# A transformer block on one core: GpSimd zeroes the exponentials of later keys in place of masks in the scores

## The chip, the core and the metric

The kernel runs on one core of one Trainium2 chip. The time is the device time in microseconds. The engines are TensorE (PE, matrix products; PEld is its weight load), VectorE (DVE), ScalarE (ACT), GpSimd (POOL) and SyncE (SP, which issues most DMAs). Each works through its own instructions in order; semaphores hold an instruction back until what it needs is done. Matrix products are written to PSUM, 8 banks here used as three pairs (`mring`) and two singles (`accp`).

## The reference

The input is x of 4 x 2048 tokens and 256 channels. A small conditioning product gives shifts, scales and gates. Then:

```python
h = _layernorm(x, axis=-1) * (1 + ca) + sa
x = x + ga * _L0_attn_ref(h, ...)        # 8 heads of 32 channels
h = _layernorm(x, axis=-1) * (1 + cb) + sb
x = x + gb * _L0_ffn_ref(h, ...)         # 2 shared and 16 routed experts, 4 per token
```

and in the attention, what bears on the change:

```python
scores = jnp.where(causal[None, None], scores, -jnp.inf)
scores = scores + head_scales[None, :, None, None] * geo
attn = jax.nn.softmax(scores, axis=-1)
out = jnp.einsum('bhqk,bhkd->bqhd', attn, v)
```

A query sees its own key and earlier ones. The extra term `geo` is a product of a projection of q and one of k, which the kernel folds into the key weights.

## The kernel before, in words

Queries are taken in 16 blocks of 512 (`QB`), four blocks to a sequence; block i has place qb = i % 4 in its sequence, so it meets qb + 1 blocks of keys. Heads are taken in two groups of four (`NQ`), and the four heads of a group lie in the four row or column quarters of TensorE, so their products run side by side.

Attention goes over the scores twice. First come the maxima (`max_steps`, lines 418 to 474), always one block ahead: `ps` is scores with queries on partitions, VectorE adds `cmask` to its last 128 columns and takes row maxima into `parts`; these are negated, cut into three bf16 pieces and turned into `mT` by TensorE (`pr`).

Then come the sums (`sum_steps`, lines 663 to 750), tile by tile of 128 keys (`kb`). `probabilities(kb)` computes `st`, scores with keys on partitions, into two pairs of PSUM banks, two heads in each, and adds the negated maxima by a product with `unit3`. In the last four key tiles, those on the diagonal, keys later than a query must vanish: there, in lines 702 to 710, four more products of `ident_b` with `kmask` (-1e30 where the key is later) are added to 128 columns of each head. A diagonal tile is computed from column `lo` on only, so the four are 512, 384, 256 and 128 columns wide. ScalarE takes the exponential of each pair into its half of `pt` (lines 711 to 714). `weigh(kb, s)` (lines 716 to 733) multiplies these with the values into `av` and with ones into `dv`, summed over all key tiles in the two `accp` banks. After the last tile `finish` (lines 735 to 741) copies `av` out on ScalarE (`num`) and `dv` on VectorE (`rd`), takes the reciprocal of 128x512 and multiplies, giving `oT`. `out_steps` (line 752) multiplies `oT` with the output weights.

The order of work is written out by hand. Every engine but for a few scatters keeps the order in which the program calls it (class `Pinned`, line 41; every operation is therefore recorded at line 52, and groups are told apart by the names of their tiles). In the stage of sums each step has a place on an axis counted in key tiles, and `run` sorts by it (lines 1404 to 1456):

```python
for n, (first, average, total) in enumerate(sums):
    part.append((n, first))
    part.append((n + 1.3, average))
    part.append((n + 1.6, total))
```

so TensorE takes the scores of tile n+1 ahead of the weighing of tile n. At n + 0.5 stand maxima of the next block, at n + 0.8 pieces of the expert choice, of the second layer norm (`second_norm_steps`, line 802) and of the next first norm, at n + 0.9 a `tick`. A norm has a power of -0.5 on GpSimd (`rsb`, waiting for VectorE), four scalings on VectorE (`xnb`), and eight multiplications or additions on GpSimd (`modulate`, line 807) with a store to `h2d` from GpSimd's queue behind them. A `tick` issues one indirect DMA from GpSimd: a scatter of a row tile to its experts' places (`xg`) or a gather back (`got`); each waits for the last instruction that ScalarE had been given (`paced`, line 496). Between two stages of sums, `fill_in` (line 515) interleaves projections (`pta`, `ppq`, `ppk`, `pv`), the turned hidden states (`ptb`), the shared experts (`pu_-2`, `pd_s`), the routed experts' tiles (`px`, `pu`, `py`) and more maxima with estimated durations; `tail` places the output products (`po`) last. After block 15 the last two blocks go through all experts densely, between the last routed tiles (lines 1464 to 1499).

Of the kernel before, what the change touches and what calls it, by code (L numbers as in the profile page):

```python
# [92 lines left out]
def adaln_block_kernel(  # L93
# [103 lines left out]
    for k in range(KC):  # L197
# [5 lines left out]
    make_identity(tc.nc, ident)  # L203
    cmask = const.tile([P, P], F32, tag="cmask", name="cmask")
    make_causal_mask(tc.nc, cmask, MASK)
    kmask = const.tile([P, P], BF16, tag="kmask", name="kmask")
    nc.gpsimd.memset(kmask, 0.0)
    nc.gpsimd.affine_select(
        out=kmask,
        in_=kmask,  # L210
        pattern=[[1, P]],
        compare_op=ALU.is_ge,
        fill=MASK,
        base=0,
        channel_multiplier=-1,
    )
    ident_b = const.tile([P, P], BF16, tag="ident_b", name="ident_b")
    nc.vector.tensor_copy(ident_b, ident)
    c_pair = cmask.unsqueeze(1).broadcast_to([P, 2, P])
# [325 lines left out]
    def merged(one, other):  # L545

        placed = []
        for pieces in (one, other):
            at, total = 0.0, sum(us for us, _ in pieces)
            for us, step in pieces:  # L550
                placed.append(((at + us / 2) / total, (us, step)))
                at += us
        return [p for _, p in sorted(placed, key=lambda p: p[0])]
# [102 lines left out]
        left = fill_in(merged(project_steps(2), gates_to_come[4:]), tops[:10])  # L656
        rest = tops[10:]

    probs = ctx.enter_context(tc.tile_pool(name="probs", bufs=2))
    tiles = ctx.enter_context(tc.tile_pool(name="tiles", bufs=2))  # L660
    kept = ctx.enter_context(tc.tile_pool(name="kept", bufs=3))

    def sum_steps(i, g, oT):

        qb = i % NB
        nkb = (qb + 1) * TT
        qT, mT = qTs[i], mTs[i, g]
        sums = []
        pts = {}

        def keys(kb):
            return (i - qb + kb // TT) % SLOTS, kb % TT

        def left(kb):
            return max(0, kb - qb * TT) * P

        def probabilities(kb):
            lo = left(kb)
            slot, n = keys(kb)
            halves = [pair(f"st{i}_{g}_{kb}_{a}") for a in range(2)]  # L680
            heads = [both[:, u, :] for both in halves for u in range(2)]
            for h in range(4):
                r = G * h
                nc.tensor.matmul(
                    heads[h][:, lo:],
                    lhsT=kT[r : r + G, slot, g, n * P : (n + 1) * P],
                    rhs=qT[r : r + G, g, lo:],
                    start=True,
                    stop=False,
                    tile_position=(r, 0),  # L690
                )
            for h in range(4):
                r = G * h
                nc.tensor.matmul(
                    heads[h][:, lo:],
                    lhsT=unit3[r : r + 3, :],
                    rhs=mT[r : r + 3, lo:],
                    start=False,
                    stop=(kb < qb * TT),
                    tile_position=(r, 0),  # L700
                )
            if kb >= qb * TT:
                for h in range(4):
                    nc.tensor.matmul(
                        heads[h][:, lo : lo + P],
                        lhsT=ident_b,
                        rhs=kmask,
                        start=False,
                        stop=True,
                    )  # L710
            pt = probs.tile([P, 4, QB], F32, tag="pt", name=f"p{i}_{g}_{kb}")
            for a, both in enumerate(halves):
                nc.scalar.activation(pt[:, 2 * a : 2 * a + 2, lo:], both[:, :, lo:], AF.Exp)
            pts[kb] = pt

        def weigh(kb, s):
            if kb == 0:
                sums.append(accp.tile([P, QB], F32, tag="acc", name=f"{'ad'[s]}v{i}_{g}"))
            lo = left(kb)
            slot, n = keys(kb)  # L720
            for h in range(4):
                r = G * h
                c0 = g * P + r
                nc.tensor.matmul(
                    sums[s][r : r + G, lo:],
                    lhsT=ones if s else vA[:, slot, n, c0 : c0 + G],
                    rhs=pts[kb][:, h, lo:],
                    start=(kb == 0),
                    stop=(kb == nkb - 1),
                    tile_position=(0, r),  # L730
                )
            if s and kb == nkb - 1:
                finish()

        def finish():
            rd = once.tile([P, QB], F32, tag="rd", name=f"rd{i}_{g}")
            num = once.tile([P, QB], F32, tag="num", name=f"num{i}_{g}")
            nc.scalar.copy(num, sums[0])
            nc.vector.tensor_copy(rd, sums[1])
            nc.vector.reciprocal(rd, rd)  # L740
            nc.vector.tensor_tensor(oT[:, g, :], num, rd, ALU.mult)

        return [
            [
                lambda kb=kb: probabilities(kb),
                lambda kb=kb: weigh(kb, 0),
                lambda kb=kb: weigh(kb, 1),
            ]
            for kb in range(nkb)
        ]  # L750

    def out_steps(i, oT):

# [208 lines left out]
    def place_steps(group):  # L962
# [18 lines left out]

        def owners():
            shape = [P, MAXT, R]
            past = once.tile(shape, BF16, tag="num", name=f"past{n}")
            nc.vector.tensor_tensor(
                past,
                tile_no.unsqueeze(2).broadcast_to(shape),
# [352 lines left out]
    def free(steps):  # L1340
        return [(0.001, s) for s in steps]

    oT = None
    filled = None
    for i in range(NBLK):
        b, qb = i // NB, i % NB
# [3 lines left out]
        if i:  # L1350
# [17 lines left out]
                mid = turns[:2] + ups + turns[2:]  # L1368
            if soon and later:
                mid += project_steps(later[0])  # L1370
            ends = [s for two in zip(downs, outs) for s in two] if downs else outs
            at = max(6, len(mid) - len(ends))
            tail = merged(mid[at:], ends) if mid[at:] else ends
            mid = mid[:at] + tail
            tops = [] if last else maxima(i + 1)
            state["pairs"] = not last
            own = sum(us for us, _ in lead + mid)
# [23 lines left out]
        if i == 0:  # L1401
            load_gates(0)
        oT = once.tile([P, KC, QB], F32, tag="oT", name=f"oT{i}")
        sums = [s for g in range(NQ) for s in sum_steps(i, g, oT)]
        assert len(sums) == ks
        part = []
        for n, (first, average, total) in enumerate(sums):
            part.append((n, first))
            part.append((n + 1.3, average))
            part.append((n + 1.6, total))  # L1410
        for n, (_, ss, turn) in enumerate(rest):
# [69 lines left out]
    more, much, others = dense_steps(j)  # L1481
    choice = free(choice_steps(i, None))
    outs = out_steps(j, oT)
    begin = turn_steps(i) + outs[:1] + choice[:2] + outs[1:] + ups
    begin += choice[2:3] + downs[:1] + choice[3:] + downs[1:] + free(second_norm_steps(j))
    fill_in(begin + in_turn(pairs[:1]), pace=1.3, add=True)
    while scatters:
        tick()
    tiles_of(filled)
    choice = free(choice_steps(j, None))  # L1490
    late = turn_steps(j) + choice + more
    rest = take_tiles(1e9)
    amid = in_turn(pairs[1:6])
    fill_in(merged(rest[:30], amid[:9]) + merged(rest[30:], amid[9:] + late), pace=2.4, add=True)
    fill_in(in_turn(pairs[6:]) + much + in_turn(others), pace=1.6, add=True)
    while ready or sums_due:
        tick()
# [44 lines left out]
```

## Time and profile before

| | us |
|---|---|
| median of 3 runs (lowest, highest) | 2557.42 (2553.51, 2558.43) |
| the profiled execution | 2559.8 |
| its span, first to last instruction | 2558.1 |
| stage of sums, block 7 (16 key tiles, two groups) | 990.7 to 1101.1 |
| end of the last stage of sums | 2281.8 |

Work by kind, from the groups of the profile (busy us):

| TensorE | | other engines | |
|---|---|---|---|
| st, scores for the sums | 421.0 | VectorE, row maxima | 662.4 |
| ps, scores for the maxima | 387.8 | ScalarE, exponentials | 538.4 |
| av and dv | 312.5 and 303.3 | GpSimd, gathers | 219.5 |
| the maxima added to st | 162.3 | GpSimd, scatters | 213.2 |

In the profile's lines, a group is named line, engine, operation, out<-in, shape and count; then busy time, mean ns of one, and the idle time of the engine just before these instructions with what ended it. A timeline's line has start and length in us first. "PEclk" is the granted share of TensorE's clock. The mean clock of the profiled execution was 0.954.

### The profile page before, as it was taken

The numbers are of one execution on the slowest core, as the hardware profiler recorded it, in microseconds if no ns is written. First come the engines' busy times: TensorE is split into PE (matmuls) and PEld (weight loads), VectorE is DVE, ScalarE is ACT, GpSimd is POOL, SyncE is SP. The second block draws the span as 40 slices with busy tenths as digits, with TensorE's granted clock in tenths as the row PEclk, the third lists the DMA queues.
The fourth block names the chain that finished last, engine by engine and source line by source line (L and its number), as shares of the span: only waits on it lengthen the run. The fifth ranks groups of instructions, "written<-read, shape, count | busy, mean of one in ns | idle before, by whom it ended". The sixth has DMA issues, their size and how long they took to land.

```text
span 2558.1 us, 42345 instructions
## 1 busy us (share of the span) xinstructions
PE 2386.6 (93%) x16961; PEld 1165.1 (46%) x16961; DVE 1405.7 (55%) x2609; ACT 977.6 (38%) x1372; POOL 701.4 (27%) x740
## 2 busy tenths in 40 slices
PE   7999999999999899999999999999898999997987
PEld 4443424345554223355654335254545643345754
DVE  5576665526666855347565566346664564422235
ACT  2223233543433234544343344643344345542320
POOL 3201010411133144202015332401442025543234
PEclk9889899999999899999999999998999999998999
DMA  2300401434432112223742235233636843247943
GB/s 87 118 1 9 148 9 42 153 127 149 154 118 63 44 58 81 75 75 101 228 136 79 73 108 173 75 101 100 214 122 215 260 144 98 89 145 264 313 135 111
DMA packets 219701, 306.90 MB, mean 120 GB/s; under 512 B 18544, under 2 KB 158832, under 8 KB 219504
## 3 DMA queue, kind: packets, MB, share of 16 engines
q1 hardware_dynamic: 192720, 228.89, 27.4%
q0 software_dynamic: 25536, 73.43, 9.1%
q8 instruction: 134, 2.20, 0.4%
q10 hardware_dynamic: 1248, 1.86, 0.2%
q14 instruction: 63, 0.52, 0.1%
HBM read 193.49 MB, written 114.82 MB: 121 GB/s over the span
## 4 chain that ended last, share of the span: by engine, by line
PE 75%; DVE 12%; ACT 4%; issue 4%; POOL 2%; DMA 2%; SPq 0%; POOLq 0%; ACTq 0%; DVEq 0%
PE st L52 15%; PE ps L52 12%; PE av L52 9%; PE dv L52 8%; PE pu L52 7%; PE py L52 5%; DVE parts L52 4%; PE po L52 3%; PE ppq L52 2%; PE pv L52 2%; PE px L52 2%; PE ppk L52 2%; DVE rd L52 2%; PE pd_s L52 1%; PE pd L52 1%
## 5 line engine op out<-in xcount | busy, mean ns | idle before, releaser
L52 DVE TENSOR_REDUCE parts<-ps 128x2 f32<-128x1024 f32 (+3 forms) x640 | 662.4, 1062 | 348.6 <-PE ps L52 339.6
L52 ACT ACTIVATE p<-st 128x1024 f32<-128x1024 f32 (+3 forms) x640 | 538.4, 893 | 652.8 <-PE st L52 652.5
L52 PE MATMUL st<-qT,kv 32*128 32x512 f32 (+3 forms) x2560 | 421.0, 594 | 32.8 <-DVE parts L52 21.0
L52 PE MATMUL ps<-kv,qT 32*128 32x512 f32 (+3 forms) x2560 | 387.8, 608 | 16.9 <-DVE parts L52 9.7
L52 POOL DMA_INDIRECT got<-yg,at x224 | 219.5, 980 | 399.7 <-ACT p L52 134.1
L52 PE MATMUL av<-p,kv 128*32 128x512 f32 (+3 forms) x2560 | 312.5, 561 | 4.6 <-DVE rd L52 4.6
L52 PE MATMUL dv<-p,ones 128*32 128x512 f32 (+3 forms) x2560 | 303.3, 546 | 0.0
L72 POOL DMA_INDIRECT xg<-rows,at x219 | 213.2, 974 | 266.9 <-ACT p L52 109.7
L52 PEld LDWEIGHTS st<-qT,kv 32*128 32x128 f32 x2560 | 141.0, 189 | 295.8 <-issue 209.2
L52 DVE TENSOR_TENSOR ps<-ps,cmask 128x256 f32<-128x256 f32 x256 | 109.3, 427 | 266.3 <-PE ps L52 245.9
L52 PEld LDWEIGHTS ps<-kv,qT 32*128 32x128 f32 x2560 | 127.8, 192 | 207.1 <-issue 112.9
L52 POOL TENSOR_TENSOR x<-x,tmps 128x512 f32<-128x512 f32 x28 | 35.4, 1263 | 623.1 <-DVE tmps L52 623.0
L52 PE MATMUL py<-wt,tact 128*128 128x256 f32 x608 | 163.8, 403 | 7.7 <-ACT xt L52 3.5
L52 PEld LDWEIGHTS pu<-xt,wt 128*128 128x128 f32 x1216 | 150.5, 197 | 29.5 <-issue 11.5
L52 PE MATMUL pu<-xt,wt 128*128 128x128 f32 x1216 | 158.3, 284 | 4.8 <-DMA wt<-experts 3.7
L52 PE MATMUL st<-mT,unit 3*128 3x512 bf16 (+3 forms) x1280 | 162.3, 353 | 0.0
L52 PEld LDWEIGHTS dv<-p,ones 128*32 128x32 f32 x2560 | 74.0, 111 | 173.9 <-issue 167.0
L52 DVE SCALAR_TENSOR_TENSOR sum<-got,weight,sum 128x256 f32<-128x256 f32 x168 | 82.9, 494 | 123.3 <-DMA got<-yg,at 119.5
L52 ACT COPY y<-py 128x512 f32<-128x512 f32 x152 | 89.0, 586 | 155.0 <-PE py L52 154.4
L52 PEld LDWEIGHTS py<-wt,tact 128*128 128x128 f32 x608 | 109.8, 195 | 57.6 <-issue 15.2
L52 ACT COPY xt<-px 128x512 f32<-128x512 f32 x152 | 86.9, 586 | 101.1 <-PE px L52 100.5
L52 PEld LDWEIGHTS av<-p,kv 128*32 128x32 f32 x2560 | 53.8, 109 | 140.1 <-issue 118.7
(287 smaller groups left out, 2425.9 us busy)
## 6 DMA issues: line engine op xcount, KB each, us to landing
wt<-experts SPq DMA_DIRECT2D x304, 256.0 KB, 4.3
xr<-xg SPq DMA_DIRECT2D x76, 512.0 KB, 4.6
yg<-y SPq DMA_DIRECT2D x76, 512.0 KB, 3.5
xg<-zeros SPq DMA_DIRECT2D x16, 1024.0 KB, 10.0
xin<-in_x SPq DMA_DIRECT2D x16, 512.0 KB, 6.2
x<-in_x SPq DMA_DIRECT2D x16, 512.0 KB, 4.5
h2d<-xnb POOLq DMA_DIRECT2D x14, 512.0 KB
pre<-x POOLq DMA_DIRECT2D x14, 512.0 KB, 3.4
```

The lines of the kernel that those rows point to most:

```text
L52: made = call(*args, **kwargs)
L72: made = call()
```

## The change

1. `kmask` and its four products in each diagonal tile are gone. In their place GpSimd sets the exponentials of later keys to 0 in SBUF: `mask(kb)` runs one `affine_select` for each half of a diagonal tile, on 128 partitions by two heads by 128 columns, 256 in all, at place n + 0.7.
2. The probabilities of a tile are two tiles of two heads each, in 5 buffers, where there was one of four heads in 2 buffers. The experts' activations, which share the tag `pt`, have 5 buffers too.
3. The order of key tiles: the first three diagonal tiles each stand ahead of a third of the other tiles, and the fourth is last. In blocks with qb = 0 there are diagonal tiles only.
4. The copies `num` and `rd` are issued at the last weighing of each, and reciprocal and product come in four pieces of 128 columns: for the first head group among the second one's tiles, for the second among the first pieces of the following fill.
5. `past` takes a buffer of tag `y` in place of `num`'s.
6. At the end, after block 15, the second norm of the last block comes behind the remaining scatters instead of ahead of them, and the last block's choice has its first step ahead of the shared experts' first products and its others behind.

The diff, cut to its core:

```diff
@@ -656,7 +645,7 @@
-    probs = ctx.enter_context(tc.tile_pool(name="probs", bufs=2))
+    probs = ctx.enter_context(tc.tile_pool(name="probs", bufs=5))
...
+        full, edge = list(range(qb * TT)), list(range(qb * TT, nkb))
+        order = edge
+        if qb:
+            cut = [0, (len(full) + 2) // 3, (2 * len(full) + 2) // 3, len(full)]
+            order = [k for n in range(3) for k in edge[n : n + 1] + full[cut[n] : cut[n + 1]]]
+            order += edge[3:]
...
-            if kb >= qb * TT:
-                for h in range(4):
-                    nc.tensor.matmul(
-                        heads[h][:, lo : lo + P],
-                        lhsT=ident_b,
-                        rhs=kmask,
-                        start=False,
-                        stop=True,
-                    )
-            pt = probs.tile([P, 4, QB], F32, tag="pt", name=f"p{i}_{g}_{kb}")
+            pts[kb] = []
             for a, both in enumerate(halves):
-                nc.scalar.activation(pt[:, 2 * a : 2 * a + 2, lo:], both[:, :, lo:], AF.Exp)
-            pts[kb] = pt
+                pt = probs.tile([P, 2, QB], F32, tag="pt", name=f"p{i}_{g}_{kb}_{a}")
+                nc.scalar.activation(pt[:, :, lo:], both[:, :, lo:], AF.Exp)
+                pts[kb].append(pt)
+
+        def mask(kb):
+
+            lo = left(kb)
+            for pt in pts[kb]:
+                nc.gpsimd.affine_select(
+                    out=pt[:, :, lo : lo + P],
+                    in_=pt[:, :, lo : lo + P],
+                    pattern=[[0, 2], [1, P]],
+                    compare_op=ALU.is_ge,
+                    fill=0.0,
+                    base=0,
+                    channel_multiplier=-1,
+                )
...
-            if s and kb == nkb - 1:
-                finish()
...
+            if last and s:
+                held["rd"] = once.tile([P, QB], F32, tag="rd", name=f"rd{i}_{g}")
+                nc.vector.tensor_copy(held["rd"], sums[1])
+            elif last:
+                held["num"] = once.tile([P, QB], F32, tag="num", name=f"num{i}_{g}")
+                nc.scalar.copy(held["num"], sums[0])
+
+        def divide(t):
+            own = slice(t * P, (t + 1) * P)
+            rd = held["rd"]
+            nc.vector.reciprocal(rd[:, own], rd[:, own])
+            nc.vector.tensor_tensor(oT[:, g, own], held["num"][:, own], rd[:, own], ALU.mult)
...
+            for n, s in enumerate(ends):
+                (lead or mid).insert(2 * n + 1, (0.001, s))
...
+        part = [(ks // NQ + 1.05 + 0.8 * n, s) for n, s in enumerate(divided)]
+        for n, (first, mask, average, total) in enumerate(sums + more):
             part.append((n, first))
+            if mask is not None:
+                part.append((n + 0.7, mask))
             part.append((n + 1.3, average))
             part.append((n + 1.6, total))
...
-    begin += choice[2:3] + downs[:1] + choice[3:] + downs[1:] + free(second_norm_steps(j))
+    begin += choice[2:3] + downs[:1] + choice[3:] + downs[1:]
...
-    late = turn_steps(j) + choice + more
+    norms = second_norm_steps(j)
+    turns = turn_steps(j)
+    late = turns + choice[:1] + more + choice[1:]
...
-    fill_in(merged(rest[:30], amid[:9]) + merged(rest[30:], amid[9:] + late), pace=2.4, add=True)
+    fill_in(free(norms) + merged(rest[:30], amid[:9]) + merged(rest[30:], amid[9:] + late), pace=2.4, add=True)
```

## The prediction

> **What bounds the kernel now.** I read the page's busy times first, then the costliest groups with shapes kept apart, then the gaps of TensorE (the waits by engine, the timeline around them, and the granted clock there), and last GpSimd's queue.
>
> ```profile
> PE 2386.6 (93%) x16961; PEld 1165.1 (46%) x16961; DVE 1405.7 (55%) x2609; ACT 977.6 (38%) x1372; POOL 701.4 (27%) x740
> ...
> PEclk9889899999999899999999999998999999998999
> ...
> PE 75%; DVE 12%; ACT 4%; issue 4%; POOL 2%; DMA 2%; SPq 0%; POOLq 0%; ACTq 0%; DVEq 0%
> ```
>
> TensorE is busy 93% of the span and is 75% of the chain that ended last; its own gaps between matmuls sum to 145 us in the trace. GpSimd is busy 27%. So a matmul taken away is worth its issue time, and a new wait in TensorE's stream costs its length. The groups that the change touches:
>
> ```profile
> L52 PE MATMUL st<-kmask,ident_b 128*128 128x128 bf16 x512 | 51.8, 225 | 0.0
> ...
> L52 DVE RECIPROCAL rd<-rd 128x512 f32<-128x512 f32 x32 | 107.3, 3353 | 1.1
> ...
> L52 POOL TENSOR_TENSOR xnb<-xnb,gm 128x256 f32<-128x256 f32 x128 | 93.9, 746 | 16.5 <-DVE xnb L52 5.2 <-issue 5.2 <-PE av L52 0.6
> ...
> masks.py:30 POOL TENSOR_SCALAR_AFFINE_SELECT cmask<-cmask 128x128 f32<-128x128 f32 x1 | 0.3, 287 | 0.0
> ```
>
> The first row is what goes. It is never waited for (idle before it 0.0), so it stands in the dense stream. The timeline of TensorE at one diagonal tile shows its real price:
>
> ```profile
> 1036.84 0.40 PE L52 MATMUL st<-mT,unit 3*128 3x512 bf16 x4
> 1037.16 0.40 PE L52 MATMUL st<-kmask,ident_b 128*128 128x128 bf16 x4
> 1037.49 1.06 PE L52 MATMUL av<-p,kv 128*32 128x512 f32 x8
> ```
>
> From 1037.16 to 1037.49 is 0.33 us; busy time overlaps its neighbours, so 0.33 and not 0.40 is what is saved.
>
> **The change part by part.**
>
> *Masks out of the scores.* 128 diagonal tiles (16 blocks, 2 head groups, 4 tiles), 0.33 us from the first mask matmul to the next instruction, near the same each time: 42.9 us of TensorE. All of it is on the path. Diagonal exponentials start 0.33 us sooner; that is not counted again.
>
> *256 selects on GpSimd.* No row shows 128x2x128. The same operation took 287 ns on 128x128; doubled, 0.57 us. Taking off the 98 ns that a one-element memset takes on GpSimd gives 0.48. I take 0.5: about 1 us for a tile's two, 128 us in all on an engine that is idle 73% of the time. That by itself costs nothing. What can cost is that av now waits for GpSimd instead of ScalarE. Behind av in TensorE's queue stand dv, the next scores and everything else. The room is read where it is tightest, at the first tile of a group:
>
> ```profile
> 1049.79 1.94 ACT L52 ACTIVATE p<-st 128x1024 f32<-128x1024 f32 x2 [1.73 <-PE st L52]
> ...
> 1052.14 1.06 PE L52 MATMUL av<-p,kv 128*32 128x512 f32 x8
> ```
>
> The second exponential ends at 1051.73, av starts at 1052.14, and its matmuls on the second half at about 1052.60: 0.87 us for one select of 0.5 us. It just fits, because the halves are now tiles of their own and the first half's select runs beside the second exponential. In the middle of a group the same distance is 1.50 us or more in nine tiles of ten. So a free GpSimd costs TensorE nothing. The cover is gone where GpSimd is not free: it works in order, and selects stand behind norms, scatters and gathers. The changed program's GpSimd order shows where. In block 5 two gathers, eight xnb multiplications, the h2d store and one gather stand between the selects of the third and fourth diagonal tiles, two tiles apart. The same run of work in the trace:
>
> ```profile
> 759.51 1.54 POOL L52 TENSOR_TENSOR xnb<-xnb,gm 128x256 f32<-128x256 f32 x2
> 761.21 0.99 POOL L52 DMA_INDIRECT got<-yg,at  x1 [0.15 <-issue]
> 762.51 0.95 POOL L52 DMA_INDIRECT got<-yg,at  x1 [0.30 <-issue]
> 763.89 4.98 POOL L52 TENSOR_TENSOR xnb<-xnb,gm 128x256 f32<-128x256 f32 x6 [0.43 <-DVE xnb L52]
> 769.17 0.85 POOL L52 DMA_DIRECT2D h2d<-xnb  x1 [0.30 <-POOL xnb L52]
> ```
>
> With the third tile's selects put in and another gather after the store, the fourth tile's first select is done at about 772.4 by these durations; its av started at 768.0 in the trace: some 4 us. Block 13 has the same pattern, 4 us. In blocks 4 and 8 the rsb power waits for VectorE until 649.9 and 1203.5, with the third tile's select behind it and two xnb more ahead of the fourth's: 2.5 us each. In block 12 rsb came at 1793.2, and the last select now stands behind it; the fill after it waited 3.9 us for VectorE anyway, so 3 us net. Block 9 has two scatters ahead of the second group's first select: 1 us; block 1: 0.5. In the nine others four or five tiles lie between diagonal ones and absorb such runs: 0.7 each, 6.3. Sum 24 us. Bounds: 0 if all is absorbed, not below, since a wait can't speed TensorE; 60 if each of 32 groups loses nearly 2 us.
>
> *What a gap costs beyond itself.* Here a page and a row disagree. The Trainium skill, page "TensorE: Matmul & The Clock Gate", section "What's actually happening", lets TensorE drop to half clock after an idle window of some 3.4 us; by it a 2 us wait costs 2 us. The trace:
>
> ```profile
> 927.29 0.91 PE L52 MATMUL st<-qT,kv 32*128 32x512 f32 x2 [1.99 <-DVE parts L52]
> ```
>
> and the busy times by stretch around it (the column before the last two is the granted clock):
>
> ```profile
> 900.00:927.00 27.00, 25.19 (x228) 8.55 (x224) 14.72 (x16) 9.64 (x14) 14.78 (x17) 1.00 0.22 74
> 927.00:935.00 8.00, 7.71 (x36) 1.62 (x40) 2.77 (x5) 1.94 (x2) 0.97 (x1) 0.57 0.06 18
> ```
>
> After a gap of 1.99 us the clock is 0.57 for 8 us. There are 33 half-clock stretches, 236 us, in which st takes 1056 ns instead of 588, so 118 us are lost; over 145 us of gaps that is 0.8 us per us. I multiply gaps by 1.8: the selects' 24 us become 43; by the page they would stay 24.
>
> A second rule speaks against the change: "SBUF — State Buffer", section "SBUF: two separate sides", has VectorE's operations on two SBUF inputs and GpSimd's hold one port pair against each other for a whole instruction. The trace agrees: rpr<-log,rmx takes 224 ns, and about 1260 in 5 of 16 cases, one of them beside GpSimd's 1.25 us x<-x,tmp at 438.05. By the rule each select may hold such an operation up 0.5 us or be held up itself. The maxima read PSUM and fall outside it; selects fill a tenth of the attention's time, so I put nothing on the path and up to 15 us in the range.
>
> *Quotients in pieces.* 192 more VectorE instructions at some 160 ns of fixed cost (a reduction takes 1221 ns on 1024 elements, 693 on 512): 31 us, covered by VectorE's 45% idle time; without that cover, 1 us per group. The gain: a reciprocal of 3.35 us with its copy and product no longer holds the maxima up in one lump. Ten TensorE gaps follow these lumps (133, 374, 771, 777, 925, 1206, 1481, 1793, 2128 and 2286 us), 21.7 us in all, 39 with the clock. The copy out of PSUM stays and the sum of work grows, so I take 60%: 23 us. Bounds 0 and 39.
>
> *Diagonal tiles apart.* Narrow tiles no longer follow one another, so maxima are spread better over TensorE's time; of 20 us of other waits for parts perhaps 5 go. Counted in the range only.
>
> *At the end.* The second norm leaves the place ahead of the last four scatters. They ran at 2309.8, after 7.1 us of rsb and xnb, and px waited 9.4 us for the rows. The scatters still wait for a Gelu that ends at 2305.8: 4 to 5 us, 8 with the clock. The later choice keeps its chain of exponential, top values and gate behind the wait, so its 6.4 us gap stays.
>
> *At nothing:* five half tiles for two whole ones (each tile's reuse still lies two tiles back), past in y's buffers (5 times; a late y store would cost its few us), the earlier num copy, and the missing kmask setup (0.5 us at the start).
>
> Sum: 42.9 + 23 + 8 - 43 = 31 us off the profiled execution's 2559.8, which stands 2.4 us above the median of 2557.4: 2526.
>
> **Rivals.** *(1) GpSimd's queue becomes the bound of diagonal tiles, slower.* If av waits for a select behind norms or indirect DMAs, at 2.5 us x 1.8 = 4.5 us a time, the 74 us gained are gone at 16 such waits, one per block. At 24 waits it costs 108: 2557.4 + 34 = 2591. For it: in-order GpSimd and rsb's dependence on VectorE. Against it: in nine blocks the diagonal tiles are far apart. Chance 0.24. *(2) Smoothing doesn't come:* VectorE's waits only move, leaving 42.9 + 8 - 43 = 8 us: 2549. For it: VectorE gets no less work. Chance 0.19, nearly half of it within 0.2%. *(3) Waits are absorbed:* a stall lets VectorE catch up and stands in place of a later gap, so only 10 us of the 43 remain and the quotients give 39: 42.9 + 39 + 8 - 10 = 80, 2477. Chance 0.15. My forecast has 0.42.
>
> The range: the forecast's terms alone give 2500 to 2552; it is drawn out to rivals 1 and 3, 2484 to 2592. Faster than 0.2% (5 us, about what a measurement of this kernel can tell from no change): 0.67; within it 0.08; slower 0.25.
>
> **What would show it.** No kmask row; TensorE's busy time down by about 50 us; some 128 us of selects at 0.5 us each. "PE av <- POOL p" among the waits, 20 to 25 us, mostly in blocks 4, 5, 8, 12 and 13. Waits for rd and parts down by about 13 us. The px wait at the end near 5 us. A mean clock near 0.954. I am wrong if av's wait for GpSimd is over 40 us, or a select takes 0.8 us or more, or the mean clock falls under 0.945.

## The result, and the profile after

The changed kernel took 2587.37 us (median of 4 runs, 2581.54 to 2589.83) beside 2557.53 us of the kernel before (4 runs): a ratio of 1.0113, 95% interval 1.0092 to 1.0134. It is slower by 30 us where I had put 31 us of gain; that lies inside my range, 4 us from the 2591 of rival 1. The profiled execution is 2589.53 us with a span of 2587.8 us.

The experiments ran later, in five rounds, each on a chip of another number (0, 2, 5, 13 and 15); which chip the first pair had is not on record. There the two kernels stand closer: the changed kernel, repeated in two of the rounds, is at 1.0011 (0.9997 to 1.0026) and 1.0016 (1.0001 to 1.0032). It takes the same 2590 us there, but the kernel before has a median of 2582 to 2587 us in all five rounds. So a loss of 11 parts in a thousand was seen in the first pair alone, and where an expectation speaks of "the chip of the experiments", five are meant. Every ratio of an experiment is to runs of the kernel before in the same round, beside it; the quotient of the two medians can differ from it by up to 0.002.

From the page of the changed kernel: busy times, the granted clock in 40 slices, and the chain that ended last by engine.

```profile
PE 2391.7 (92%) x16449; PEld 1156.1 (45%) x16449; DVE 1436.2 (56%) x2801; ACT 977.8 (38%) x1372; POOL 805.4 (31%) x994
...
PEclk9889899999999899999989899998998999899999
...
PE 72%; DVE 10%; POOL 6%; issue 5%; DMA 4%; ACT 3%; SPq 0%; POOLq 0%; ACTq 0%; DVEq 0%
```

512 matmuls are gone and TensorE is busy 5 us longer, not 50 us shorter. Its gaps sum to 170.3 us (145.5 before), and the granted clock is half for 311.6 us (236.4). GpSimd has risen from 2% to 6% of the chain. The groups that answer to those shown of before:

```profile
L52 PE MATMUL av<-p,kv 128*32 128x512 f32 (+3 forms) x2560 | 336.7, 580 | 56.1 <-POOL p L52 54.4
...
L52 POOL TENSOR_SCALAR_AFFINE_SELECT p<-p 128x256 f32<-128x256 f32 x256 | 105.1, 423 | 364.3 <-ACT p L52 362.3
```

A select takes 0.42 us (I had 0.5), 105 us in all. But before av TensorE now stands still for 54.4 us, and GpSimd is what ends it. Among TensorE's waits by releaser it is the largest by far (columns: us in total, times, longest):

```profile
PE av L52 <- POOL p L52: 54.4, 21, 5.9
PE st L52 <- DVE parts L52: 11.4, 18, 2.3
PE ps L52 <- DVE parts L52: 11.1, 24, 1.6
...
PE px L52 <- DMA xr<-xg: 9.0, 2, 4.7
```

The longest is in block 15, one of those that I thought safe. The timeline of ScalarE, GpSimd and TensorE there (start, duration, instruction, idle time before it and what ended it; some instructions left out):

```profile
2249.90 0.97 POOL L72 DMA_INDIRECT xg<-rows,at  x1 [0.30 <-issue]
...
2250.88 4.51 POOL L52 TENSOR_TENSOR xnb<-xnb,gm 128x256 f32<-128x256 f32 x6
...
2252.49 1.94 ACT L52 ACTIVATE p<-st 128x1024 f32<-128x1024 f32 x2 [2.06 <-PE st L52]
2255.54 1.01 POOL L72 DMA_INDIRECT xg<-rows,at  x1 [0.15 <-issue]
2256.86 0.97 POOL L72 DMA_INDIRECT xg<-rows,at  x1 [0.30 <-issue]
2257.84 0.78 POOL L52 TENSOR_SCALAR_AFFINE_SELECT p<-p 128x256 f32<-128x256 f32 x2
2258.32 0.19 PEld L52 LDWEIGHTS av<-p,kv 128*32 128x32 f32 x4 [6.62 <-POOL p L52]
2258.32 1.43 PE L52 MATMUL av<-p,kv 128*32 128x256 f32 x8 [5.91 <-POOL p L52]
```

Six multiplications of the norm and three scatters, eight microseconds of GpSimd, stand ahead of a select of 0.4 us, and av starts 0.48 us after that select has begun. Then av takes 1.43 us where it takes 0.64 at full clock. The busy times by stretch around it (the column before the last two is the granted clock) show why:

```profile
2240.00:2250.00 10.00, 10.00 (x100) 2.81 (x96) 5.50 (x17) 6.46 (x8) 3.30 (x4) 1.00 0.08 27
2250.00:2256.00 6.00, 2.41 (x24) 0.56 (x16) 0.00 (x0) 2.38 (x3) 5.60 (x8) 0.87 0.13 44
2256.00:2266.00 10.00, 7.68 (x48) 2.39 (x52) 0.00 (x0) 1.94 (x2) 6.65 (x9) 0.57 0.19 66
```

### The profile page after: what moved, and what is told of

Its sections match the earlier page's. It is cut to its first block, busy times and chain, and to the rows that moved or that the text cites. A ratio compares the mean times of both kernels' runs of the same rounds, so it can differ in the third digit from the quotient of the medians.

```text
span 2587.8 us, 42082 instructions
## 1 busy us (share of the span) xinstructions
PE 2391.7 (92%) x16449; PEld 1156.1 (45%) x16449; DVE 1436.2 (56%) x2801; ACT 977.8 (38%) x1372; POOL 805.4 (31%) x994
## 4 chain that ended last, share of the span: by engine, by line
PE 72%; DVE 10%; POOL 6%; issue 5%; DMA 4%; ACT 3%; SPq 0%; POOLq 0%; ACTq 0%; DVEq 0%
PE st L52 12%; PE ps L52 12%; PE av L52 9%; PE dv L52 7%; PE pu L52 7%; PE py L52 5%; DVE parts L52 4%; PE po L52 3%; PE ppq L52 2%; PE pv L52 2%; PE px L52 2%; PE ppk L52 2%; POOL xnb L52 2%; POOL got L52 2%; PE pd L52 2%
## 5 line engine op out<-in xcount | busy, mean ns | idle before, releaser
L52 PE MATMUL ps<-kv,qT 32*128 32x512 f32 (+3 forms) x2560 | 399.2, 610 | 19.0 <-DVE parts L52 11.1
L52 PE MATMUL av<-p,kv 128*32 128x512 f32 (+3 forms) x2560 | 336.7, 580 | 56.1 <-POOL p L52 54.4
L52 PE MATMUL dv<-p,ones 128*32 128x512 f32 (+3 forms) x2560 | 322.6, 559 | 0.0
L52 POOL TENSOR_SCALAR_AFFINE_SELECT p<-p 128x256 f32<-128x256 f32 x256 | 105.1, 423 | 364.3 <-ACT p L52 362.3
L52 PEld LDWEIGHTS av<-p,kv 128*32 128x32 f32 x2560 | 59.0, 111 | 246.8 <-issue 161.1
L52 PEld LDWEIGHTS dv<-p,ones 128*32 128x32 f32 x2560 | 84.5, 115 | 180.7 <-issue 172.6
```

The costliest lines, as they stand in the source:

```text
L52: made = call(*args, **kwargs)
```

## The experiments

**Theory 1:** the loss is av's wait for selects that stand behind other work in GpSimd's queue, 54 us, and the half clock that follows. **Theory 2:** the order, the half tiles or the pieces cost the time. **Theory 3** came up when theory 1 had failed its first test: the products' 43 us were not on the path, since without them TensorE waits longer and its clock falls; **theory 4** is its rival, that a product costs its time. **Theory A** and **theory B** are about the 25 us that the kernel before takes more in the later rounds (each expectation says what its B is). **Theory 5**, in the last ones, says that a wait that is taken away only moves. A "late start" is an exponential that begins 2 us or more after its last score product and ScalarE's work before it have ended.

*No selects.* In the list of steps:

```diff
-                (lambda kb=kb: mask(kb)) if kb in edge else None,
+                None,
```

> The changed kernel without the 256 selects; it leaves out the zeroing of later keys in the diagonal tiles, and nothing else is different. Theory 1 (the loss is av's wait for selects that stand on GpSimd behind the second norm, stores and indirect DMAs, each wait with its stretch of half clock): the 54 us of waits and some 38 us of half clock go, so 2587 - 92 = 2495 us (2480 to 2510), no wait of av for GpSimd, mean clock 0.95 or more, half-clock stretches down from 312 us to below 240 us. Theory 2 (the new order, the half tiles or the pieces of the quotients cost the time, the selects matter little): 2550 us or more, the half-clock stretches still near 300 us.

Measured: 2584.13 us, 1.0000 (0.9985 to 1.0016). av's waits for GpSimd are gone, yet the gaps of TensorE are 166.5 us, half clock 303.6 us, and the granted clock of its runs has a median of 0.942. With neither masks nor selects the kernel is no faster than before. Theory 1's 92 us fall; what the selects cost here is 1.0011 to 1.0016 less 1.0000, some 3 to 4 us, which the intervals can't tell from nothing.

*Products instead of selects.* `kmask` and its four products back in `probabilities` as they were (`tile_no_i` goes into y's buffers to make room), `None` in place of `mask`.

> The changed kernel with the masks back in the scores as 512 products with kmask, and no selects: order of tiles, half tiles, pieces of quotients and the end as changed. The whole computation is there. Theory 1: 43 us above the kernel without selects, 2538 us (2525 to 2550), faster than before by some 20 us, which is what the pieces and the end are worth. Theory 2: 2580 us or more, slower than before although no select is left.

Measured: 2581.04 us, 0.9994 (0.9979 to 1.0009); gaps 139.5 us, half clock 235.9 us, median clock 0.954. 512 products more than the kernel above, and not slower: neither expectation (2538, or 2580 and *slower* than before) had that.

*The norm's products on VectorE.* In `modulate`:

```diff
-                nc.gpsimd.tensor_tensor(xn[:, t, :], xn[:, t, :], gm[b][:, row, :], op)
+                nc.vector.tensor_tensor(xn[:, t, :], xn[:, t, :], gm[b][:, row, :], op)
```

> The changed kernel with the second norm's multiplication and addition (the 128 xnb instructions, 94 us of GpSimd) on VectorE. Theory 1: the seven waits of 3.0 to 5.9 us behind runs of eight xnb, 31 us, go with their half clock of some 20 us; the waits for rsb stay; VectorE's own extra work gives some 5 to 10 us back: 2545 us (2530 to 2560), av's waits for GpSimd 20 us instead of 54. Theory 2: no gain, VectorE has 94 us more, 2587 to 2620 us.

Measured: 2566.45 us, 0.9945 (0.9917 to 0.9972), by the ratios 17 us below the changed kernel, where 42 were expected. The 128 instructions take 432 ns on VectorE, 744 on GpSimd. The waits alone are as expected:

```profile
PE av L52 <- POOL p L52: 22.8, 13, 5.7
```

*The norm's products spread.* `steps += [(1.0, s) for s in norm[:-TT]] + [(4.0, s) for s in norm[-TT:]]` in place of 1.0 for all.

> The changed kernel with the second norm's four multiply-and-add steps four times as far apart in the attention's order, so that in most blocks selects stand between pairs of xnb instead of behind all eight. Theory 1: half of the 31 us behind runs of xnb goes, with its clock: 2587 - 25 = 2562 us (2550 to 2575), av's waits for GpSimd 30 to 40 us. Theory 2: 2587 us within 5.

Measured: 2576.93 us, 0.9962 (0.9938 to 0.9985), waits for GpSimd 29.3 us, in place of the 51 to 54 in the three traces of the changed kernel. Same instructions on the same engine, only further apart, so a run of eight has a cost. But 22 us of waits and their clock gave 13 us, and that the cost comes through the selects is not shown: further down the norm's move gains as much in a kernel without selects.

*The two kernels once more.*

> The kernel before once more, for its trace on the chip on which the other kernels run: its median in the first four experiments was 2582 us where it had been 2557 us, with the same mean clock of 0.954. Theory A: that chip has the 25 us as late releases of exponentials beside dense runs of indirect DMAs (lags of 2 to 6 us, which the two kernels without selects show and the first trace of before does not): such lags, 20 us or more, are in this trace too. Theory B: those lags come from the new order of tiles, and this trace shows none over 2.1 us.

Measured: 2584.05 us, 1.0001 (0.9983 to 1.0018). What theory A expects is in the trace: seven exponentials beside indirect DMAs start 2.1 to 5.1 us after both their last score product and ScalarE's work before them have ended, 22 us in all (24 with one at the start of the program); the first trace of before has none beside indirect DMAs. Theory B, that they come from the new order of tiles, falls. The same place in both, end of block 9, first the record's trace of before, then this one:

```profile
1359.45 0.96 POOL L72 DMA_INDIRECT xg<-rows,at  x1 [0.30 <-ACT p L52]
...
1359.86 0.40 PE L52 MATMUL st<-kmask,ident_b 128*128 128x128 bf16 x4
...
1360.24 0.66 ACT L52 ACTIVATE p<-st 128x256 f32<-128x256 f32 x2 [1.16 <-PE st L52]
```

```profile
1368.46 0.40 PE L52 MATMUL st<-kmask,ident_b 128*128 128x128 bf16 x4
...
1369.15 0.96 POOL L72 DMA_INDIRECT xg<-rows,at  x1 [0.30 <-issue]
...
1370.42 0.96 POOL L72 DMA_INDIRECT xg<-rows,at  x1 [0.30 <-issue]
...
1371.68 0.96 POOL L72 DMA_INDIRECT xg<-rows,at  x1 [0.30 <-issue]
1373.95 0.66 ACT L52 ACTIVATE p<-st 128x256 f32<-128x256 f32 x2 [5.53 <-remote]
```

The scores end at 1368.86 and the exponential starts at 1373.95; "remote" means that the trace shows nothing that released it. The program is the same. Between the two traces TensorE's work shifts by 22 us in all, and 20 of them arise at late starts in blocks 6, 9, 14 and 15, 3 to 6 us in each; TensorE's gaps, 145.5 and 148.6 us, hardly show it; its busy time, 2386.6 and 2401.7 us, does. The two kernels above without selects have late starts too; the changed kernel, run next, has 4.5 us of them.

> The changed kernel once more, on the chip of the other experiments. If the ratio to before stays at 1.011, the selects cost only 11 parts in a thousand (29 us) against the same kernel without them, and theory 1's 92 us are wrong by two thirds. If it is above 1.025, theory 1's size stands and the chip was the difference.

Measured: 2590.12 us, 1.0011 (0.9997 to 1.0026); waits for GpSimd 51.3 us, near the 54.4 of the first trace.

*Before without masks.* The four products deleted from the kernel before.

> The kernel before without its 512 products with kmask; it leaves out the zeroing of later keys in the diagonal tiles, and nothing else is different. My prediction's term: 42.9 us, all on the path, ratio 0.983. Theory 3 (the products' time lies to a large part in waits for the exponentials, and without them TensorE waits longer and falls to half clock more often): a ratio of 0.993 or more, the gaps of TensorE up by 10 us or more and the half-clock stretches by 30 us or more.

Measured: 2580.88 us, 0.9979 (0.9961 to 0.9997): 5 us, not 42.9. Theory 3's numbers are met in the traces: gaps 180.0 us against 148.6, half clock 305.3 us against 237.3. The two executions that were profiled exaggerate it, 2588 us here beside 2578 of before; from the median clock of all runs, 0.944 and 0.951, I estimate 289 and 253 us at half clock. Before in this round, then this kernel:

```profile
PE 2401.7 (93%) x16961; PEld 1164.9 (45%) x16961; DVE 1406.8 (55%) x2609; ACT 978.5 (38%) x1372; POOL 701.7 (27%) x740
```

```profile
PE 2380.4 (92%) x16449; PEld 1144.0 (44%) x16449; DVE 1406.6 (54%) x2609; ACT 978.5 (38%) x1372; POOL 702.2 (27%) x740
```

ScalarE ends 19 of the 31 us by which the gaps grew, and VectorE most of the rest. The two waits that grew most, with products and then without (columns: us in total, times, longest):

```profile
PE st L52 <- ACT p L52: 9.0, 11, 1.6
PE pta L52 <- ACT num L52: 1.7, 4, 0.5
```

```profile
PE st L52 <- ACT p L52: 20.3, 14, 4.2
PE pta L52 <- ACT num L52: 8.9, 5, 6.2
```

The longest of them is at the end of block 9. `num` and VectorE's copy `rd` wait there, beside scatters, until 5.5 us after the last dv:

```profile
1368.83 0.48 PE L52 MATMUL dv<-p,ones 128*32 128x128 f32 x6
...
1374.84 0.58 ACT L52 COPY num<-av 128x512 f32<-128x512 f32 x1 [6.20 <-remote]
1374.93 0.69 DVE L52 COPY rd<-dv 128x512 f32<-128x512 f32 x1 [10.50 <-remote]
1375.47 1.97 PE L52 MATMUL pta<-ident,xin 128*128 128x128 f32 x8 [6.16 <-ACT num L52]
```

Another place shows a chain of known links, the end of block 4 (the rows that matter, out of VectorE's, GpSimd's and TensorE's). With products, then without:

```profile
650.74 1.01 POOL L52 TENSOR_TENSOR rsb<-rsb,half_power 128x4 f32<-128x4 f32 x1 [15.68 <-DVE rsb L52]
...
651.79 2.27 DVE L52 TENSOR_SCALAR xnb<-x,mvb,rsb 128x256 f32<-128x256 f32 x4 [1.12 <-POOL rsb L52]
...
652.12 0.40 PE L52 MATMUL dv<-p,ones 128*32 128x128 f32 x8
...
653.98 0.68 DVE L52 COPY rd<-dv 128x512 f32<-128x512 f32 x1
...
654.71 0.66 PE L52 MATMUL pta<-ident,xin 128*128 128x128 f32 x4 [1.04 <-DVE rd L52]
```

```profile
648.77 0.40 PE L52 MATMUL dv<-p,ones 128*32 128x128 f32 x8
...
649.03 1.01 POOL L52 TENSOR_TENSOR rsb<-rsb,half_power 128x4 f32<-128x4 f32 x1 [14.91 <-DVE rsb L52]
...
650.08 2.27 DVE L52 TENSOR_SCALAR xnb<-x,mvb,rsb 128x256 f32<-128x256 f32 x4 [1.12 <-POOL rsb L52]
...
652.26 0.68 DVE L52 COPY rd<-dv 128x512 f32<-128x512 f32 x1
...
653.00 0.66 PE L52 MATMUL pta<-ident,xin 128*128 128x128 f32 x4 [2.68 <-DVE rd L52]
```

The last dv comes 3.35 us earlier, pta only 1.71: the copy of `dv` stands on VectorE behind the norm's scalings, which wait for the power on GpSimd, which waits for VectorE's statistics. TensorE waits 2.68 us for it instead of 1.04. That this chain holds at other diagonal tiles is not shown.

*The selects alone.* The kernel before with `mask` and half tiles of `pt` as in the change, products out, everything else old.

> The kernel before with only the masks changed: half tiles of probabilities and the 256 selects on GpSimd, in the old order of tiles (diagonal tiles last, one after the other) and with the quotients in one piece. Theory 1: the waits grow, since four diagonal tiles in a row stand behind a run of xnb: av's waits for GpSimd 60 to 100 us, ratio 1.015 to 1.03. Theory 2 (the order or the pieces are what hurts): ratio 1.00 or less.

Measured: 2599.79 us, 1.0043 (1.0025 to 1.0061), waits for GpSimd 53.2 us. Theory 1's direction, below its size. Against the kernel without masks in the same order (0.9979) the selects, with the half tiles, cost 0.0064, 17 us, for 53 us of waits.

*Useless products, of the full array and of a quarter,* ahead of the diagonal scores in the changed kernel, which overwrite them:

```diff
+            if kb >= qb * TT:
+                for h in range(4):
+                    nc.tensor.matmul(
+                        heads[h][:, lo : lo + P], lhsT=ident_b, rhs=ident_b, start=True, stop=True
+                    )
```

The quarter has `heads[h][:G, ...]` and `lhsT=ident_b[:, :G]`.

> The changed kernel with four useless products in each diagonal tile: 128x128 of the identity, full array, written to the score tile just ahead of the scores, which overwrite them. The whole computation is there. Theory 3 (the granted clock of each 3.4 us window follows the share of the array's cells that the window before kept in use; the products with kmask were what held it up): clock back from 0.943 to 0.952, and 43 us more of TensorE's issue cost next to nothing, ratio 0.998 to 1.006. Theory 4 (the clock follows idle time alone, and a product's time is on the path): clock 0.945 or less, ratio 1.012 to 1.018.

> As the kernel with useless products, but with 32 of the 128 columns of the array: the same number of instructions over the same 128 columns of data, a quarter of the cells. Theory 3: the clock gets little from them, 0.945 or less, and their time is paid in part: ratio 1.006 to 1.016, above the full products' by 0.005 or more. Theory 4: as the full products, within 0.003.

Measured: 1.0118 (1.0091 to 1.0145) and 1.0071 (1.0051 to 1.0090), mean 227 and 224 ns a product, clock 0.948 for both, half clock 274.6 and 273.3 us against 293 to 312 in the three traces of the changed kernel. Theory 3's part about the array's cells falls: a quarter of the cells held the clock as well. About the path neither theory is met: added in front of the scores, their 43 us of issue time cost 28 and 16 us, by the ratios. So products cost more where they were added, in front of the scores of the changed kernel, than they gave where they were taken out of the kernel before; why the full ones cost more than the quarter ones stays open.

*Useless products where TensorE waits:* the kernel with the norm's products on VectorE, and in `weigh`, ahead of the first av:

```diff
+                for _ in range(0 if s else 4):
+                    nc.tensor.matmul(
+                        sums[0].rearrange("p (a b) -> p a b", a=TT),
+                        lhsT=ident_b,
+                        rhs=ident_b.unsqueeze(1).broadcast_to([P, TT, P]),
+                        start=True,
+                        stop=True,
+                    )
```

> The kernel with the second norm's products on VectorE (0.9945 of before), and ahead of the first av of each of the 32 groups four useless full-array products over 512 columns, 0.85 us, in the accumulator that av then overwrites: TensorE waits there some 0.9 to 1.6 us for the first exponentials. Theory 3: half-clock windows after these waits go, clock up by 0.003 to 0.006, ratio 0.989 to 0.993. Theory 4: the waits are filled with work but nothing is gained, 0.9945, or up to 0.9985 where the products come in the way.

Measured: 0.9972 (0.9959 to 0.9986), clock 0.953 in place of 0.9465. The clock rose as theory 3 has it, but the time did not fall. From 0.9945 it may have risen; the two intervals touch, so what is shown is that filling these waits gains nothing.

*GpSimd in step with the tiles:* products with `kmask`, no selects, and `nc.gpsimd.tensor_scalar(mark, pt[:, 0, lo : lo + 1], 1.0, None, ALU.mult)` for each half of a tile (two in each tile).

> The changed kernel with the masks as products with kmask (0.9994 of before), no selects, and instead one GpSimd instruction of one element per partition in each key tile, which reads the tile's exponentials: GpSimd can't run its indirect DMAs ahead of the attention. Theory A (dense runs of indirect DMAs delay the releases of the exponentials on this chip, 24 us in before): the lags of 2 us and more go, ratio 0.989 to 0.993. Theory B (the lags are the trace's own and cost nothing): 0.9994 within 0.002.

Measured: 0.9971 (0.9953 to 0.9990), late starts of 19.8 us. The ratio lies between the two expectations, and the late starts did not go; this says nothing on what they cost.

*The quotients alone,* and *the end alone*, each put into the kernel before as in the change.

> The kernel before with only the quotients in four pieces of 128 queries, and past in y's buffers; masks as products, old order, old end. The prediction's term: 23 us, ratio 0.991 (0.985 to 1.000). Theory 5 (a lump's wait only moves, as with the products: TensorE then waits for the sum of VectorE's work): 0.999 to 1.003, the waits for rd gone but those for parts or num up by as much.

Measured: 0.9971 (0.9957 to 0.9985), 7.5 us. TensorE's waits for rd go from 9.0 to 0.7 us, those for num rise from 3.8 to 15.7.

> The kernel before with only the end changed: the last second norm behind the last scatters and the dense block's later choice spread. The prediction's term: 8 us, ratio 0.997. From the traces: the stretch from the last copy of num to TensorE's last matmul is 260 and 257 us in the two traces of before, and 247 and 244 us with the changed end: 10 to 14 us, ratio 0.995 to 0.996. Theory 5: 1.000 within 0.002.

Measured: 0.9984 (0.9967 to 1.0000), 4 us, where the traces had promised 10 to 14.

*Two kernels meant to beat both:* products with `kmask`, order, pieces and end as changed, and the norm's products on VectorE; and the kernel before with the changed end and the norm's products on VectorE.

> The changed kernel with masks as products instead of selects (0.9994), and the second norm's products on VectorE. If the gain of the move is the selects' alone (no select stands behind xnb any more), nothing is left to gain: 0.998 to 1.002. If GpSimd's queue delays gathers and scatters in any case, 0.992 to 0.996.

Measured: 2563.63 us, 0.9910 (0.9878 to 0.9941, 5 runs): the lowest median of all, 19 us below before and 26 below the changed kernel, though its interval overlaps that of 0.9945 above.

```profile
PE 2409.6 (94%) x16961; PEld 1174.9 (46%) x16961; DVE 1462.9 (57%) x2929; ACT 978.2 (38%) x1372; POOL 607.0 (24%) x612
```

TensorE has all its products back, its gaps are 129.2 us, the least of any trace. The move gains 0.0084 here without a single select (against 0.9994, from another round), so what it gained with selects need not be theirs.

> The kernel before with the changed end and with the second norm's products on VectorE; masks as products, old order, quotients whole. Sum of the two parts where they add up: 0.995 for the end and up to 0.994 for the move, 0.989 to 0.993. If the move only helps selects: 0.995 to 0.998.

Measured: 0.9952 (0.9937 to 0.9968), at the lower end of what was expected if the move only helps selects; but there are no selects here, and against the end alone (0.9984) the move gives 0.0032, 8 us.

*Fewer scatters at a time.* In `ticks` of the kernel before, `if n % 2 and 4 * len(ready) > ks - n` without `scatters or`.

> The kernel before with one scatter, not two, at every other key tile of the attention; all else as before. Theory A (dense runs of indirect DMAs delay the exponentials' release): the late starts of 2 us and more fall from 24 us to under 12, ratio 0.992 to 0.997, if the later scatters collide with nothing else. Theory B (the late starts stand in place of other waits and cost nothing): 0.998 to 1.002, or slower where the scattered rows come late for the routed tiles (px waits for xr up by 5 us or more).

Measured: 1.0127 (1.0097 to 1.0157), late starts some 17 us, by the count that gives 22 for before. The collision that the expectation left room for: st's waits for parts go from 18.6 to 34.9 us and the routed products wait 15.8 us for weights.

```profile
PE st L52 <- DVE parts L52: 34.9, 35, 3.3
PE pu L52 <- DMA wt<-experts: 15.8, 16, 2.6
```

It says nothing on theory A.

> The changed kernel a third time. If the chip decides: 1.001 where before takes 2583 us or more, 1.011 where before takes 2557 us. If the first comparison was a chance of few runs: 1.001 to 1.005 whatever before takes.

Measured: 2589.71 us, 1.0016 (1.0001 to 1.0032), with before at 2584.58. Both readings had this for a kernel before at 2584, so it doesn't decide between them. All runs of before beside the experiments lie between 2569 and 2599 us; the 2557 us of the first pair did not come again, and so neither did its ratio.

*The late starts of all traces,* one trace to each kernel or repeat:

| traces | late starts, us |
|---|---|
| the first pair, before and after | 0 and 0 |
| later rounds, no selects, norm's products on GpSimd (8 traces) | 17 to 31 |
| later rounds, no selects, norm's products on VectorE (0.9910, 0.9952) | 10 and 3 |
| later rounds, with selects (8 traces) | 0 to 5 |

So selects and the moved products each go with fewer late starts. Where the products move in kernels without selects, 17 and 14 us of late starts go (26 to 10, 17 to 3), and 22 and 8 us of time.

## Why the prediction was wrong

**"All of it is on the path", of 42.9 us: this step failed, and the experiments show it.** Taking only the products out gives 0.0021 of 2586, 5 us (1 to 10 by the interval), and in the new order they are worth nothing (1.0000 without, 0.9994 with). The time went into new waits and into the clock: in the trace the gaps grew by 31 us, and 68 us more at half clock lose half of that, 34; by the clock of all runs it is nearer 18. One such wait is explained, the chain over VectorE and GpSimd at the end of block 4; the larger part, 17 of the 31 us, where TensorE waits for ScalarE that started late beside scatters, is seen and not explained. What I read from the row, idle before it 0.0, was that nothing holds the product up; it doesn't say that nothing holds up what comes after it. Of the first pair I have the trace only: blocks 0 to 2, which have next to no waits for selects, became 10 us shorter there, so some of the gain was had.

**"In the nine others four or five tiles lie between diagonal ones and absorb such runs: 0.7 each": failed in the trace.** Waits for GpSimd of 0.6 us and more, by block: 3 4.8, 6 3.1, 7 2.8, 14 5.0, 15 8.5 us, 24 us in five blocks that I had given 3.5. The named ones were near: 5 5.5 and 13 7.6 for 4 each, 8 3.3 and 4 0.9 for 2.5 each, 9 4.4 for 1; 12 has 7.1 for 3. The count of tiles was off too: by the order in the diff, four lie between diagonal ones only where qb = 3, two or three where qb = 2, as in blocks 6 and 14, and none in block 0. A tile in between takes 3.2 us of TensorE, but GpSimd's run had grown with it: in block 15 it takes eight, and the next diagonal select sits behind the whole of it. I looked at the distance between selects in tiles and not at what had been queued in that distance.

**The factor of 1.8 for a gap held, for those gaps.** By my count from the clock's record 24 windows of 3.41 us at half clock belong to stretches that begin behind such a wait of av, 24 x 3.41 / 2 = 41 us; (54.4 + 41) / 54.4 = 1.75. With 54.4 us in place of 24 the selects' term is 98 instead of 43, and my own sum turns to 74 - 98 = -24 us: 2581 to the 2587 measured. That is the arithmetic of rival 1, with 21 waits of 2.6 us for its 24 of 2.5. For the first pair of runs it is the reading that fits best, but it rests on the trace; where I could test, the same 51 to 53 us of waits cost 17 us in the old order and 3 to 4 in the new one, and the gains of 74 came to 17. So the nearness of this sum, and of rival 1's number, to the 2587 is luck as far as the experiments go: both of its terms are several times too large there. In them waits stand in for one another: with no select, late starts rise from 4.5 to 31 us and TensorE's waits for `num` come to 30 us (8 in the trace after).

**The quotients, 23 us, measured 7.5.** The lumps went: waits for rd and parts fell by 18.5 us in the trace after (I said 13), and reciprocals and products take 32 us more of VectorE, as worked out (31). But TensorE then waits for num.

**The end, 8 us, measured 4 (0 to 8.5).** In the trace after, px's wait is the one that I gave, 4.4 us, and the 6.25 us of the gate stay.

**The sum in the experiments:** products 0.0021, pieces 0.0029, end 0.0016, together 0.0066 or 17 us for my 74; selects 0.0064 or 17 us for my 43. That leaves nothing, where 3 to 4 us were measured. The order and the half tiles were not run by themselves. Pieces and end would put a kernel with products at 0.9955; with order and half tiles it stands at 0.9994, so these may cost some 10 us there; that is a difference of rounds and not a test. With that the sum is 1.0037, above the measured 1.001 to 1.002: the parts do not simply add. The range had a slip of its own: it was to reach rival 3, but stops at 2484, short of that rival's 2477.

**Points that held:** 0.42 us for a select, that a free GpSimd costs TensorE nothing, no sign of the port pair (the quotients' products take 319 ns with selects and 309 without, 1.3 us in all), and two of my three marks of being wrong, waits over 40 us and a clock under 0.945, were met.

**Open:** why before takes 25 us more in every later round than in the first pair. A difference of chips is one reading, but the first chip is not known and no round came back to it; something else on that first occasion is another. In the one later trace of before, the 22 us arise for the most part at late starts, as shown above. What makes them late is not known: the trace models the ends of matmuls, so it can't tell a signal that comes late from a product that ends late, and VectorE's `rd` was late along with `num`. The two attempts to take them away, GpSimd in step and fewer scatters at a time, left them in place. Most of them went where the norm's products moved, with 8 and 22 us of time, but that move takes load off GpSimd in other ways too. That the changed kernel escapes them because its selects hold TensorE in the same places anyway, and that this is why 1.011 became 1.001, is argued and not shown.

## What to carry to other kernels

That an engine is busy 93% and that a group is never waited for does not put the group's time on the path: before a gain is booked, follow what else the next wait depends on, and take the work out on the chip, which is one small edit. When a wait is handed to an in-order engine, list everything queued between two of its uses, not the distance between them. And the queue that is in the way is sometimes better shortened than routed around: here moving 94 us of norm from GpSimd to VectorE gave 8 to 22 us in three kernels, two of them without a select. And a ratio that was measured on one occasion only should be measured again before it is explained: here 1.011 came back as 1.001 and 1.002.

## What the runs showed of the hardware

The granted clock changes on a fixed grid of 3.41 us: every one of the 413 half-clock stretches in ten traces starts on a whole multiple of it, as the Trainium skill's page "TensorE: Matmul & The Clock Gate", section "What's actually happening", has it (a free-running window of 3413 ns). The idle window of that length, which the page has ahead of half clock, was not needed here. Of full-clock windows with under 0.3 us of TensorE idle, 18 of 5516 were followed by half clock; with 0.9 to 1.2 us, 39 of 160; with 1.2 to 2.0 us, 139 of 230; with 2.0 to 2.5 us, 55 of 56. Weighted by the rows and columns of the array that a matmul uses, a window under 0.35 of the array's capacity (full products of 512 columns, one every 0.43 us) was followed by half clock 355 times of 434, and one over 0.45 once in 5986; scores use 32 rows of 128. That is a count, not a test; the one test, with full and quarter products, did not bear it out. And in one trace of the kernel before the exponentials beside runs of indirect DMAs started 2 to 5 us late, in an earlier trace of the same program beside the same runs they did not.
